# Fourth score chunk of the second attention layer by half products, in a four-layer graph network on one Trainium2 core

## The chip, the core and the metric

The kernel runs on one core of a Trainium2 chip. The core has a matrix engine (TensorE, PE in the profile, with its weight loads as PEld), three engines for elementwise work (VectorE or DVE, ScalarE or ACT, GpSimd or POOL), and SyncE (SP), which here only issues DMA transfers. Sixteen DMA engines move data between the chip's large memory (HBM, "DRAM" below) and the on-chip memory (SBUF); TensorE writes its results to PSUM. Each engine runs its own instructions in their order and waits for others through semaphores.

The metric is device time in microseconds (us). Before the change it was 2243.39 us, the median of six runs from 2237.05 to 2248.49.

## The reference

A graph has N = 2708 nodes with 512 features each and a symmetric 0/1 adjacency matrix `adj`. Four layers follow each other, each of the form `x = layernorm(x + layer(x, adj))`. Layers 0, 1 and 3 multiply `adj` by the features and then by a 512 x 512 weight. Layer 2 is the one that matters here. It holds two attention layers of this form:

```python
proj = x @ W
Wh, Ws = jnp.split(proj, 2, axis=-1)
scores = Wh @ Ws.T
a = jax.nn.softmax(scores, axis=-1) * adj
out = a @ Wh
out = out + x
return jax.nn.leaky_relu(out, NEG_SLOPE)
```

The scores are dense (2708 x 2708, 512 deep), and so is the sum of the softmax. The weighing `a @ Wh` is sparse, since `adj` has some 16 neighbours a node.

## The kernel before, in words

**Layout.** Nodes stand in 22 blocks of 128 rows (the last has 20 rows), and in six column chunks `CH` of 512, 512, 512, 512, 384 and 276 columns, numbered 0 to 5; "the fourth chunk" is number 3. Chunk k of an attention layer computes the scores of all 22 row blocks against its columns, transposed: a tile `s` of 128 x 512 for every row block.

**A chunk of scores, directly.** `scores` makes a block by four matmuls of 128 x 128 by 512 columns, accumulated in PSUM; ScalarE copies the result to SBUF. Block 21 (20 rows) is done in small tiles and summed by VectorE.

**A chunk of scores by seven half products.** Where the chunk's number stands in `SEVEN` (one list for each of the two attention layers, line 507), `pair_steps` takes two row blocks at a time and makes their scores from seven products of half the depth and half the columns instead of eight (Winograd's form of Strassen's method). There are ten such pairs; block 18 (`ALONE`) and block 21 are done directly. A product is two matmuls of 256 columns (`product`). The method needs sums and differences of both sides: of the weights side they are the tiles s1, s2 and s4 of each group of blocks, of the moving side t1, t2 and t4 (`sum_moving`). In the course of this ScalarE copies six parts out of PSUM (`spx`, `spy`, `u`, `v`), and VectorE adds `u` and `v` to them (`first_block`, `second_block`). For groups 0 to 3 the sums on the weights side don't stay in SBUF: chunk 0 writes them to DRAM (`keep_sums`), and each later chunk by seven loads them again (`load_sums`, three transfers of 256 KB a group, on SP's queue). `replace` and `restore` turn one quarter of the weights in place into a difference, and back to the original when the next chunk is direct.

**What goes on beside the scores.** While the scores of chunk k are made, chunk k-1 (and what is left of chunk k-2) goes through three more steps, recorded by the loop in `layer`:

1. Softening (`soften`, called through `soften_next`): VectorE subtracts the greatest score, ScalarE takes the exponential, VectorE adds to the running sum and multiplies by the mask, and SP stores the block in a DRAM table of rows (`pairs<-s`). A chunk takes 26 steps. The table alternates between two copies, so chunk k can't be stored before chunk k-2 has been read.
2. Gathering (`fetch`): when all of a chunk's blocks are stored, GpSimd issues indirect DMAs (`g<-pairs,givers`) that bring the rows of the neighbours. A full chunk has 48 of them, each into one of ten buffers.
3. Weighing (`weigh`): TensorE multiplies the gathered weights and features (`acc<-g`), one matmul for each gather; the first of a chunk is preceded by the divisors (`den`). `end` then does the rest of the block on VectorE.

**What sets the order.** The order of issue on every engine is that of recording (class `Ordered`). A clock in the recording code (`advance`) adds up TensorE's matmuls; `weigh` records a weighing only when by this clock its gather should have landed, unless it is called with `wait=True`. In `layer`, after each block ("end") a number `many` of softening steps is recorded, and one more step at each "mid" of `pair_steps`. With `old` for chunk k-1:

```python
many = 2 if self.to_soften[:1] == [old] else 3
if ch.seven:
    many = (many - 1 if n % 2 else many - 2) if k > 1 else 0
```

After the last chunk of the second attention layer the loop goes on with layer 3 (`early`, the `fill` of `layer`): eight stretches of adjacency matmuls (`acc<-m,xh` and `acc<-m,xl`). Before its first two, `early` calls `need(GROUPS[t + 2][1] - 1)`, which asks for finished rows 8 to 11 and then 12 to 15 and records weighings with `wait=True` until they are there. Rows 12 to 15 are those of chunk 3. They are then loaded from DRAM by `load_rows`, while rows 16 to 21 are taken from the SBUF tiles in `made`.

Of the kernel before, what the change touches and what calls it, by code (L numbers as in the profile page):

```python
# [27 lines left out]
CH = [(0, 512), (512, 512), (1024, 512), (1536, 512), (2048, 384), (2432, 276)]  # L28

GROUPS = [(0, 4), (4, 8), (8, 12), (12, 16), (16, 19), (19, 22)]  # L30
# [473 lines left out]
APART = 3  # L504
SOFT = NB + APART + 1
ALONE = 18
SEVEN = ([0,1,2,3],[0,1,2])
PROJECTED = [0, 1]


# [42 lines left out]
class Fast:  # L553
# [91 lines left out]
    def early(self, run):  # L645

        seq = run.seq
        yield True
        self.load(*seq[0])
        yield True  # L650
        self.load(*seq[1])
        self.prepare(*seq[0])
        yield True
        for t in range(4 * TWO):
            ly, k, g = seq[t]

            for later in seq[t + 2 if t == 0 else t + 6 : t + 7]:
                self.load_bytes(*later)
            if t < 2:
                self.attention.need(GROUPS[t + 2][1] - 1)  # L660
            self.load(*seq[t + 2])
            if t == 4:
                self.load_weights(ly)
            if t == 4 * TWO - 1:
                self.attention.need(GROUPS[4][1] - 1)
                for j in range(*GROUPS[4]):
                    ly.rows[j] = self.attention.made[j]
            self.prepare(*seq[t + 1])
            if g == 3:
                ly.begun[k] = []  # L670
            for n, j in enumerate(range(*GROUPS[g])):
                if t == 0:
                    self.multiply(ly, k, g, [j])
                else:
                    self.multiply(ly, k, g, ds=[n])
                if g == 3:
                    b = self.page(f"begun{k}_{n}")
                    self.nc.scalar.copy(b[:, : CH[k][1]], ly.acc[k][n][:, : CH[k][1]])
                    ly.begun[k].append(b)
                self.attention.advance(2 * cost(CH[k][1]))  # L680
                yield True
# [169 lines left out]
    def load(self, ly, k, g):  # L851

        c0, cw = CH[k]
        if (k, g) in ly.loaded:
            return
        ly.loaded.add((k, g))
        js = range(*GROUPS[g])
        if ly.number == 0:
            tiles = []
            for j in js:  # L860
                if k == 0:
                    self.load_rows(ly, j)
                at = self.wide(f"at{ly.number}_{k}_{j}")
                tiles.append(at)
                if j < NB - 1:
                    self.nc.sync.dma_start(
                        at[:, :cw], self.k.adj_t[bass.ts(j, P), c0 : c0 + cw]
                    )
                    continue

                few = self.k.adj_t[j * P : j * P + QW, c0 : c0 + cw]
                for d in range(DC):
                    self.nc.sync.dma_start(at[d * QW : (d + 1) * QW, :cw], few)
            ly.done["at", k, g] = tiles
        else:
            self.load_bytes(ly, k, g)
        if k == 0 and ly.number == 3 and g < 4:
            for j in range(*GROUPS[g]):
                self.load_rows(ly, j)
        if ly.number == 0 and g == (2 if k else 4):  # L880
            xt = [self.page(f"xt{k}_{c}") for c in range(DC)]
            for c in range(DC):
                self.nc.gpsimd.dma_start(xt[c][:, :cw], self.k.x_t[:, c, c0 : c0 + cw])
            ly.done["xt", k] = xt
# [744 lines left out]
class Attention:  # L1629
# [470 lines left out]
    def pair_steps(self, ch):  # L2100
# [52 lines left out]
        for n, p in enumerate(pairs):  # L2153
            self.replace(ch.ly, p[0])
            if ch.k == 0 and p[0] in groups and p[1] == 0:
                self.keep_sums(ch.ly, p[0])
            if ch.k and p[1] == 0 and p[0] + 1 in groups:
                self.load_sums(ch.ly, p[0] + 1)
            t = begin(n, p)
            ahead(t)  # L2160
            if old:
                first_block(old)
            yield "mid"
            one(t)
            if older:
                four(older)
            if following and p == pairs[-2]:
                self.load_sums(ch.ly, 0)
            yield "end"
            if old:  # L2170
                seven(old)
            yield "mid"
            six(t)
            if old:
                second_block(old)
            older, old = old, t
            yield "end"
# [371 lines left out]
    def layer(self, ly, chunks, fill):  # L2549
        f = self.f  # L2550
        self.chunks, self.made = chunks, {}
        for k, ch in enumerate(chunks):
# [3 lines left out]
            n = -1  # L2556
            for what in self.walk(ch):
                if what == "mid":
                    self.soften_next()
                    self.weigh()  # L2560
                    continue
                n += 1
                if old and n < old.masks_ahead:
                    self.load_mask(old, n)
                if not following and n > NB - 1 - ch.masks_ahead:
                    self.load_mask(ch, n - NB + ch.masks_ahead)
                if old and n < 2:
                    self.greatest(old, last=n == 1)
                if old and n == 2:
                    self.shift_rows(old)  # L2570
                many = 2 if self.to_soften[:1] == [old] else 3
                if ch.seven:
                    many = (many - 1 if n % 2 else many - 2) if k > 1 else 0
                for _ in range(many):
                    self.soften_next()
                f.beat()
                if k == 0 and n < NB:
                    self.copy_z(ly, n)
                if n == 14 and k:
                    f.packed(k - 1)  # L2580
                if following and n == 15:
                    self.load_moving(following)
                if following and following.seven and n == 18:
                    self.sum_moving(following)
                if not following and n in (5, 11, 19):
                    next(fill)
                if ch.seven and not following.seven and n >= 7 and n % 4 == 3:
                    self.restore(ly, n // 4 - 1)
                if not ch.seven and n == 1:
                    for i in sorted(ly.sums):  # L2590
                        self.restore(ly, i)
                self.greatest(ch)

                for _ in range(3):
                    if not self.weigh():
                        break
                late = k == 2 or ly.number == 0 and k == len(CH) - 1
                if old and n == (6 if late else 4):
                    self.shift_columns(old)
                    self.to_soften.append(old)  # L2600
        assert not self.to_soften
# [129 lines left out]
```

## Time and profile before

| What | us |
|---|---|
| median of six runs | 2243.39 |
| profiled execution | 2240.0 |
| its span, first to last instruction | 2238.3 |
| TensorE busy in it | 2186.1 (98%) |
| VectorE busy | 1627.2 (73%) |
| ScalarE busy | 825.7 (37%) |
| GpSimd busy | 719.3 (32%) |

Stages of the two attention layers in that execution, by the first score product of each chunk (us from the start of the span):

| Chunk | first layer | second layer | scores by seven in (first, second) |
|---|---|---|---|
| 0 | 735.03 | 1414.95 | both |
| 1 | 801.59 | 1479.13 | both |
| 2 | 867.52 | 1545.06 | both |
| 3 | 962.31 | 1640.18 | first only |
| 4 | 1064.94 | 1745.53 | neither |
| 5 | 1145.02 | 1829.29 | neither |
| work after the scores | 1204.19 | 1892.18 | |

The last weighing of the second layer ends at 2039.6.

How to read the profile: its rows group instructions by engine and by the names of the tiles that are written and read (`out<-in`). One f32 matmul appears as two records, so `x40` of scores are twenty matmuls. A matmul's busy time includes waiting once it has begun, so the distance between starts is used for prices. Nearly all rows have line L71, that of the recording helper; the names tell them apart.

### The profile page before, as it was taken

The page shows a single profiled execution, that of the slowest core. Times are in us where ns is not written, and L with a number is a line of the kernel's source. Part 1 is how long each engine was busy: PE and PEld are TensorE (multiplying, and loading weights), DVE is VectorE, ACT ScalarE, POOL GpSimd, SP SyncE. Part 2 cuts the span into 40 slices and gives each one's busy share as a digit, 9 for nine tenths or more (in the row PEclk, how much of TensorE's full clock was granted, in tenths as well). Part 3 has the DMA queues.
Part 4 walks back from the last instruction along what each step waited for, and adds up shares of the span by engine and source line. Part 5 has one row for each costly group of instructions (what it writes and reads, how often), then busy time and mean ns, then how long its engine had stood idle before and what let it go on. Part 6 is the DMA issues. An engine that isn't in the chain of part 4 may idle for free. (4 is left out here: it accounts for less than half of the span.)

```text
span 2238.3 us, 30631 instructions
## 1 busy us (share of the span) xinstructions
PE 2186.1 (98%) x10012; PEld 1572.6 (70%) x10012; DVE 1627.2 (73%) x3425; ACT 825.7 (37%) x1855; POOL 719.3 (32%) x827
## 2 busy tenths in 40 slices
PE   9999999999999999999999999999999999899997
PEld 6777778889887887666555666887643455477896
DVE  6777888897887869888867732459988688445744
ACT  7444363333333345343322422335432223442121
POOL 2333431111000000646566542000556556443000
PEclk9999999999999999999999999999999999999999
DMA  9976762222412855999899974764999899884221
GB/s 348 279 205 173 201 182 68 86 86 91 154 58 96 288 176 154 343 306 338 263 359 338 320 239 156 241 230 148 320 309 313 277 337 312 321 267 129 94 87 43
DMA packets 311566, 488.95 MB, mean 218 GB/s; under 512 B 37498, under 2 KB 178074, under 8 KB 311396
## 3 DMA queue, kind: packets, MB, share of 16 engines
q1 hardware_dynamic: 242740, 271.74, 36.8%
q0 software_dynamic: 68656, 215.15, 29.6%
q8 instruction: 81, 1.33, 0.2%
q14 instruction: 89, 0.73, 0.1%
HBM read 357.28 MB, written 162.76 MB: 232 GB/s over the span
## 5 line engine op out<-in xcount | busy, mean ns | idle before, releaser
L71 POOL DMA_INDIRECT g<-pairs,givers x510 | 537.5, 1054 | 799.4 <-DMA pairs<-s 224.1
L71 PE MATMUL acc<-m,xh 128*128 128x512 f32 (+4 forms) x1584 | 563.4, 377 | 1.0 <-issue 1.0
L71 PE MATMUL acc<-m,xl 128*128 128x512 f32 (+4 forms) x1584 | 549.7, 365 | 3.6 <-DVE xl L71 3.6
L71 PEld LDWEIGHTS acc<-m,xh 128*128 128x128 f32 (+1 forms) x1584 | 288.4, 188 | 59.8 <-issue 19.1
L71 PEld LDWEIGHTS acc<-m,xl 128*128 128x128 f32 (+1 forms) x1584 | 288.7, 188 | 46.0 <-DVE xl L71 4.1
L71 PE MATMUL sp<-xs,wst_sb 128*128 128x384 f32 (+2 forms) x960 | 300.0, 485 | 0.0
L71 PE MATMUL acc<-g 128*32 128x512 f32 (+1 forms) x1020 | 277.6, 611 | 9.2 <-DMA g<-pairs,givers 4.5
L71 PEld LDWEIGHTS sp<-xs,wst_sb 128*128 128x128 f32 x960 | 165.7, 182 | 131.1 <-issue 70.2
L71 ACT CAST m<-at 128x512 fp32r<-128x512 uint8 (+5 forms) x396 | 201.5, 567 | 115.3 <-DMA at<-mask 47.0
L71 PEld LDWEIGHTS acc<-g 128*32 128x32 f32 (+1 forms) x1020 | 77.2, 135 | 138.3 <-issue 108.6
L71 DVE TENSOR_TENSOR s<-s,a 128x512 f32<-128x512 f32 (+3 forms) x264 | 166.3, 630 | 9.1
L71 DVE TENSOR_TENSOR sum<-sum,s 128x512 f32<-128x512 f32 (+4 forms) x252 | 156.6, 621 | 10.2 <-issue 6.0
L71 DVE TENSOR_TENSOR s<-s,shift 128x512 f32<-128x512 f32 (+3 forms) x264 | 161.4, 620 | 1.9 <-ACT rs_t L71 1.1
L71 DVE TENSOR_TENSOR top<-top,s 128x512 f32<-128x512 f32 (+3 forms) x240 | 149.4, 623 | 15.7 <-ACT s L71 10.1
L71 ACT ACTIVATE s<-s 128x512 f32<-128x512 f32 (+3 forms) x264 | 146.5, 580 | 37.5 <-DVE s L71 22.6
L71 ACT COPY s<-sp 128x384 f32<-128x384 f32 (+2 forms) x112 | 52.7, 472 | 267.6 <-PE sp L71 176.7
L71 ACT COPY s<-spx 128x256 f32<-128x256 f32 x210 | 77.9, 373 | 144.6 <-PE spx L71 115.2
L71 POOL DMA_DIRECT2D x<-o x44 | 25.6, 589 | 324.5 <-DVE o L71 281.0
L71 PE MATMUL spx<-xs,wst_sb 128*128 128x256 f32 x400 | 103.2, 382 | 4.6 <-issue 2.1
L71 DVE SCALAR_TENSOR_TENSOR xr<-acc,rden,xr 128x512 f32<-128x512 f32 (+1 forms) x44 | 32.7, 744 | 93.1 <-PE acc L71 61.4
L71 PE MATMUL mm<-w,ht 128*128 128x512 f32 (+1 forms) x240 | 100.1, 594 | 0.0
L71 PEld LDWEIGHTS spx<-xs,wst_sb 128*128 128x128 f32 x400 | 75.1, 190 | 26.5 <-issue 11.4
(349 smaller groups left out, 3320.5 us busy)
## 6 DMA issues: line engine op xcount, KB each, us to landing
pairs<-s SPq DMA_DIRECT2D x168, 256.0 KB
at<-in_adj_t SPq DMA_DIRECT2D x84, 256.0 KB
pairs<-pairs SPq DMA_DIRECT2D x42, 512.0 KB
s<-sums SPq DMA_DIRECT2D x60, 256.0 KB
xres<-x POOLq DMA_DIRECT2D x44, 256.0 KB
x<-o POOLq DMA_DIRECT2D x43, 256.0 KB
pairs<-z_sb SPq DMA_DIRECT2D x42, 256.0 KB
pairs<-pairs SPq DMA_DIRECT2D x42, 256.0 KB
```

The lines of the kernel that those rows point to most:

```text
L71: ins = call(*args, **kw)
```

## The change

`SEVEN` gets chunk 3 for the second attention layer as well. Besides, group 1 of the sums is loaded at the end of the chunk before and no longer at the beginning of the chunk that uses it; the number of softening steps after a block is 2 for all chunks, and 1 or 2 in turn in the last one; the shift of chunk 4 is recorded two blocks earlier in the last chunk of the first layer (block 4, not 6); and rows 12 to 15 of layer 3 are taken from `made`, not loaded.

```diff
-SEVEN = ([0,1,2,3],[0,1,2])
+SEVEN = ([0,1,2,3],[0,1,2,3])
...
             if t < 2:
                 self.attention.need(GROUPS[t + 2][1] - 1)
+            if t == 1:
+                for j in range(*GROUPS[3]):
+                    ly.rows[j] = self.attention.made[j]
             self.load(*seq[t + 2])
...
-        if k == 0 and ly.number == 3 and g < 4:
+        if k == 0 and ly.number == 3 and g < 3:
             for j in range(*GROUPS[g]):
                 self.load_rows(ly, j)
...
-            if ch.k and p[1] == 0 and p[0] + 1 in groups:
+            if ch.k and p[1] == 0 and p[0] > 0 and p[0] + 1 in groups:
                 self.load_sums(ch.ly, p[0] + 1)
...
-            if following and p == pairs[-2]:
-                self.load_sums(ch.ly, 0)
+            if following and p in pairs[-2:]:
+                self.load_sums(ch.ly, pairs.index(p) - len(pairs) + 2)
...
-                many = 2 if self.to_soften[:1] == [old] else 3
+                many = 1 + n % 2 if k == len(CH) - 1 else 2
                 if ch.seven:
                     many = (many - 1 if n % 2 else many - 2) if k > 1 else 0
...
-                late = k == 2 or ly.number == 0 and k == len(CH) - 1
-                if old and n == (6 if late else 4):
+                if old and n == (6 if k == 2 else 4):
                     self.shift_columns(old)
                     self.to_soften.append(old)
```

The instructions of the two programs, counted by chunk in the order in which they stand: in the second layer's chunk 3, 80 score matmuls of 512 columns go and 140 of 256 columns come. Weighings recorded in a chunk's stretch change like this:

| Stretch | first layer, before and after | second layer, before and after |
|---|---|---|
| chunk 2 | 38, 26 | 38, 26 |
| chunk 3 | 54, 62 | 58, 62 |
| chunk 4 | 42, 46 | 48, 46 |
| chunk 5 | 30, 30 | 38, 30 |
| after the scores | 91, 91 | 73, 91 |

In the second layer, 10 weighings of chunk 3 stood after the scores; now 28 do. The 16 weighings of chunk 4 that `need` records with `wait=True` stand right behind them in both programs. The divisors of chunk 3, which open its weighing, stood behind 28 score matmuls of chunk 5 and now stand behind 52.

## The prediction

> **What bounds the kernel now.** I read the page first, then busy time by stage, then waits and the timeline of the stages that change.
>
> ```profile
> span 2238.3 us, 30631 instructions
> ...
> PE 2186.1 (98%) x10012; PEld 1572.6 (70%) x10012; DVE 1627.2 (73%) x3425; ACT 825.7 (37%) x1855; POOL 719.3 (32%) x827
> ...
> PEclk9999999999999999999999999999999999999999
> DMA  9976762222412855999899974764999899884221
> ```
>
> TensorE is busy 98% of the span, so fewer matmuls should shorten it. But DMA is at 9 tenths exactly in the two stretches of attention, so a gather may be what TensorE waits for there. The stages (start:end, length, then PE, PEld, DVE, ACT, POOL busy, clock, DMA share, GB/s) separate these. First the second layer's chunks 1, 2 and 3, then the first layer's chunk 3, which is already made by seven products:
>
> ```profile
> 1479.13:1545.06 65.93, 65.93 (x305) 55.55 (x304) 52.67 (x91) 31.12 (x75) 0.00 (x0) 1.00 0.44 139
> 1545.06:1640.18 95.12, 87.72 (x389) 61.98 (x388) 85.95 (x145) 38.59 (x91) 45.69 (x43) 1.00 0.85 286
> 1640.18:1745.53 105.35, 104.87 (x313) 42.08 (x312) 89.58 (x151) 28.70 (x51) 60.67 (x57) 1.00 0.94 307
> ```
> ```profile
> 962.31:1064.94 102.63, 97.62 (x437) 65.99 (x436) 83.58 (x139) 38.10 (x90) 55.20 (x53) 1.00 0.97 322
> ```
>
> Chunk 1 is pure TensorE. Chunk 3 made directly leaves TensorE idle for 0.5 us; made by seven products, in the first layer, for 5.0. Chunk 2 idles 7.4. Its two longest waits, in TensorE's timeline:
>
> ```profile
> 1566.14 1.13 PE L71 MATMUL spx<-t,wst_sb 128*128 128x256 f32 x4 [1.75 <-ACT v L71]
> 1579.68 1.13 PE L71 MATMUL spy<-t,s 128*128 128x256 f32 x4 [2.47 <-DMA s<-sums]
> ```
>
> The last stretch that matters lies after the scores, where `need` records weighings without regard to their gathers:
>
> ```profile
> 1909.35 5.37 PE L71 MATMUL acc<-g 128*128 128x512 f32 x8 [1.00 <-DMA g<-pairs,givers]
> 1915.14 6.27 PE L71 MATMUL acc<-g 128*32 128x512 f32 x12 [0.42 <-issue]
> ...
> 1928.08 1.13 PE L71 MATMUL acc<-g 128*128 128x512 f32 x2 [0.28 <-issue]
> ```
>
> From 1909.35 to 1928.64 TensorE does only the 16 forced weighings of chunk 4. Eight whole ones at 0.89 (1680.06 to 1682.72 for three) and two lists of four quarters at 1.0 are 9.1 us; the stretch takes 19.3. Ten us are lost here and count as busy. The sixteenth gather is issued at 1922.1: **this point is set by the stream of gathers, not by TensorE.** Afterwards adjacency matmuls cover nearly everything to the end.
>
> **The change, part by part.** The sums are made against the profiled execution, 2240.0 us (span 2238.3 and 1.7 around it), which lies 3.4 under the median of 2243.39.
>
> *Matmuls.* A direct score matmul costs 0.860 us (1682.72 to 1686.16 for four), a half one 0.432 (1549.36 to 1550.22 for two). 80 x 0.860 = 68.8 go, 140 x 0.432 = 60.5 come: **-8.3 us of TensorE's work**, all in chunk 3 of the second layer.
>
> Here a rule speaks against the change. The row first: half matmuls stand 0.216 us apart a record, and the weight load of each takes 0.190 beside it. The Trainium skill, "TensorE: Matmul & The Clock Gate", section "Back-to-back issue gap", says that in a stream of weight loads and matmuls both set the spacing, and that with few columns the formula for a single matmul counts too little (81 ns against 56 at 128 columns). An estimate from that page, 25 ns on each of 280 records, is 7 us, and the gain would be 1.3. The rows show no such surcharge, so -8.3 stands.
>
> *What seven products need on other engines in that chunk.* VectorE gets 10 additions `s<-s,u` at 0.684, 9 `s<-s,v` at 0.419 and two subtractions more: 6.8 + 3.8 + 0.8 = 11.4 us. ScalarE exchanges 19 copies of 512 columns at 0.586 for 29 `s<-spx`, 9 `v`, 10 `s<-spy` at 0.373 and 10 `u` at 0.593: +12.7 us on 28.7 busy of 105, which is hidden. VectorE's is hidden only if it can run near full: 89.6 busy and some 10.7 more (busy time there is 0.935 of the sum of its durations) are 100 in a stage of 100. The first layer's chunk 3 shows what this costs, 5.0 of TensorE idle in place of 0.5: **+4.5**, bounded by 0 below and 10 above (VectorE at the 90% of chunk 2: 100/0.90 = 111 for the stage).
>
> *Sums.* Twelve loads of 256 KB more, 3.1 MB; at the stage's 307 GB/s that is 10 us of all sixteen engines, in a stage at 0.94 of them. SP issues them between the pair stores. Bounds: 0, if they fall into the 6% that is free, to +9, if every gather moves. I take +1, since the first layer's chunk 3 carries the same load at 0.97 and its gathers go on.
>
> *Sums a chunk ahead.* The wait of 2.47 above is for group 2. In SP's order its three loads stood behind eight pair stores, and SP waits 36.6 us for VectorE in that stage; the group 1 loads, now gone to the chunk before, and the slower softening leave four of those stores behind it instead of ahead. **-2.5** in the second layer, **-0.7** in the first (the same wait is 0.74 there). If the loads are still late, 0.
>
> *Fewer softening steps.* No step goes away; they are moved. In chunk 2 of both layers VectorE gets relief where it is densest (98% busy from 1550 to 1600). TensorE's other idle time there, 4.9 and 5.5 us, should halve: **-2.5 in each layer** (0 to -5). The price is that chunk 0's gathers begin later: its divisors stand behind 104 score matmuls of chunk 2, not 82, and 12 weighings move to chunk 3. GpSimd idles 10 us between chunks 0 and 1, so this lag has room; without the room it costs up to 5. Queued behind the moved steps are only the pair stores on SP and the gathers on GpSimd.
>
> *Order in chunk 5.* Here the gain is handed back. The divisors of chunk 3, and so the weighing that frees the ten gather buffers, stand behind 52 score matmuls of chunk 5, not 28: 24 x 0.478 (1863.95 to 1867.77 for eight) = 11.5 us later in TensorE's work. So -8.3 before it becomes **+3.2** there; with -5.0 from chunk 2, +4.5 and +1, the first weighing of chunk 3 comes about 3.7 later than at 1843.46. From the gather behind it (1844.84) to the sixteenth of chunk 4 the stream takes 77.3 us for 52, 1.49 each. An unhindered gather takes 1.26 (0.95 and 0.30 idle), a mean one 1.37 (207 from 1575.7 to 1922.1, less 62 us in which GpSimd waited for stores and buffers). Now that the weighings are forced, buffers come free at once. At 1.37 it is 71.2, **-6.1**; at 1.26, -11.8; at 1.49, 0. The forced point comes 6.1 - 3.7 = **2.4 us earlier**, and TensorE waits longer in front of it: what was gained in matmuls is spent there.
>
> *Rows 12 to 15 from SBUF.* Four loads of 256 KB go. VectorE waited 4.13 us for them at 1947.20, but TensorE had adjacency matmuls: 0, at best -2. *Shift two blocks earlier* in the first layer's last chunk: 2 blocks of slack for VectorE, 0.
>
> **Sum.** Second layer -2.4; first layer -0.7 - 2.5 = -3.2, which its tail keeps, as its projections follow on TensorE without forced weighings. Together -5.6: 2234.4 for an execution like the profiled one, **2238 us** on the scale of the median.
>
> **Rivals.**
>
> 1. *The whole saving arrives.* If gathers keep 1.26 and chunk 3 costs no new idle time, the forced point moves by 3.2 - 5.0 - 11.8 = -13.6; with -3.2 of the first layer -16.8: **2227**. For it: ten us of forced waiting is room for TensorE. Against: DMA share of 0.94 there.
> 2. *VectorE becomes the bound in chunk 3* (slower). If it gets no further than 90%, the stage takes 111 and not 101; chunk 2's pair stores, chunk 3's and then every gather move with it, and the forced point comes at 10 - 2.4 = +7.6. The first layer's gain then falls too, for the same reason, to about 0: with a gather or two more in the tail **2252**. It decides from the point at which the stage exceeds its old 105. For it: 85.95 of 95.12 in the densest stage. Against: 98% over 50 us.
> 3. *Nothing happens to the time.* The later gathers of chunk 0 cost what the shorter waits gain, in both layers, and the forced point stays: **2243**. For it: TensorE loses its time at gathers whatever it does before.
>
> **Chances.** Forecast 0.41 (2232 to 2244), rival 1 0.27 (2222 to 2232), rival 2 0.17 (2250 to 2258), rival 3 0.15 (2240 to 2248). A measurement of this kernel can tell about 0.3% from no change, 6.7 us; 2236.7 is the border. Faster is rival 1 and a little over a third of the forecast, 0.27 + 0.16 = 0.43; slower rival 2 with 0.17; the same 0.40. The range reaches into both rivals: 2225 to 2252.
>
> **What would show it.** Right: the row `spy<-t,s` loses its wait for sums; the second layer's chunk 3 takes 98 to 104 us with TensorE idle some 5 of it; the chunk 3 divisors come within 5 us of the old place after 1414.95; the forced stretch begins earlier and is longer. Wrong: chunk 3 above 105 with VectorE over 95% (rival 2), gathers of chunk 3 and 4 at 1.26 and the forced stretch shorter (rival 1), or the first layer no shorter from 735.03 to 1414.95 (its -3.2).

## The result and the profile after

The changed kernel takes 2259.13 us (median of 35 runs, 2239.4 to 2274.41) where the kernel before takes 2244.94 on the same chip (72 runs, 2233.64 to 2265.08): a ratio of 1.0063, 95% interval 1.005 to 1.0076. It is **14 us slower**, and lies above the range of the prediction (2225 to 2252). The profiled execution took 2258.96, its span 2257.2.

The page of the changed kernel, the lines that answer to those shown of before:

```profile
span 2257.2 us, 30965 instructions
...
PE 2186.8 (97%) x10132; PEld 1601.8 (71%) x10132; DVE 1637.4 (73%) x3453; ACT 836.6 (37%) x1895; POOL 720.1 (32%) x827
...
PEclk9999999999999999999999999999999999999999
DMA  9976752223322945999989873855989899874221
```

TensorE is as busy as before (2186.1 there), although the change takes 8 us of matmuls away. So some 9 us more of it are waits that count as busy, or matmuls at half clock (the mean granted clock is 0.990 here and 0.995 before), and outside its busy time it stands still for 70.4 us in place of 52.2 (span less busy). Busy time by stage, in the columns of the prediction: the second layer's chunks 2 and 3, then the first layer's chunk 3.

```profile
1549.93:1643.74 93.81, 82.63 (x365) 61.38 (x364) 86.46 (x148) 37.84 (x90) 35.49 (x34) 0.95 0.81 273
1643.74:1749.38 105.64, 100.66 (x437) 65.56 (x436) 90.98 (x158) 39.31 (x89) 64.54 (x61) 1.00 0.93 315
951.11:1059.47 108.36, 102.57 (x454) 67.72 (x452) 91.51 (x150) 40.16 (x93) 68.07 (x61) 0.98 0.98 332
```

Chunk 3 of the second layer takes 105.6 as before, with 5.0 of TensorE idle. Chunk 2 now idles 11.2 (7.4 before) and has half clock in it. TensorE's timeline there; a row without brackets had no wait:

```profile
1579.23 1.03 PE L71 MATMUL spy<-t,s 128*128 128x256 f32 x4
...
1635.55 2.07 PE L71 MATMUL spy<-xs,wst_sb 128*128 128x256 f32 x4 [10.96 <-ACT s L71]
```

The wait for sums (2.47 at `spy<-t,s`) is gone, and a wait of 11 us for ScalarE has come. Yet chunks 4 and 5 are shorter, and the second layer's scores end 467.8 us after its start, 6.7 earlier than before. All of it is lost behind the scores. First TensorE waits for VectorE's `xl` (the part of the features that `xh` leaves), in front of the second adjacency matmul; at this place there was no such wait before:

```profile
1894.61 0.79 PE L71 MATMUL acc<-m,xl 128*128 128x512 f32 x1 [6.73 <-DVE xl L71]
```

Then comes the stretch in which it does nothing but weighings. Its first row before, then the changed kernel:

```profile
1904.62 2.97 PE L71 MATMUL acc<-g 128*32 128x512 f32 x8
```
```profile
1908.61 4.00 PE L71 MATMUL acc<-g 128*32 128x512 f32 x16
1913.25 6.41 PE L71 MATMUL acc<-g 128*128 128x512 f32 x12 [0.64 <-issue]
...
1926.94 1.05 PE L71 MATMUL acc<-g 128*32 128x512 f32 x2 [1.91 <-DMA g<-pairs,givers]
...
1938.42 2.04 PE L71 MATMUL acc<-g 128*32 128x512 f32 x4 [1.66 <-DMA g<-pairs,givers]
1940.67 7.49 PE L71 MATMUL acc<-g 128*32 128x512 f32 x16 [0.20 <-issue]
```

Before, it lasted 24.0 us, from 489.7 to 513.7 after the layer's start (19.3 of them for the 16 weighings of chunk 4); now it lasts 39.0, from 488.8 to 527.8. The last weighing ends 638.6 after the layer's start, where it was 624.6; what follows takes 198.8 and 198.7. So 14 us come in between the second layer's start and its last weighing (the other 5 of these two executions lie ahead of that start), and the question is why the gathers are late.

Followed back, the gathers are late from chunk 2's first on. That one needs chunk 2's last block, the one of 20 rows, to be softened and stored. First the kernel before: the last multiplication by the mask on VectorE, then the gather on GpSimd.

```profile
1727.54 0.68 DVE L71 TENSOR_TENSOR s<-s,a 20x512 f32<-20x512 f32 x1
```
```profile
1742.19 0.95 POOL L71 DMA_INDIRECT g<-pairs,givers  x1 [7.37 <-PE acc L71]
```

The same two of the changed kernel:

```profile
1756.73 0.68 DVE L71 TENSOR_TENSOR s<-s,a 20x512 f32<-20x512 f32 x1
```
```profile
1760.42 0.95 POOL L71 DMA_INDIRECT g<-pairs,givers  x1 [7.08 <-DMA pairs<-s]
```

Counted from each layer's start (1414.95 and 1419.82), this last multiplication began at 312.6 and now begins at 336.9. Before, GpSimd waited for a weighing to free its buffer (`PE acc`), with the chunk long softened: the gather came 14.6 us after the multiplication. Now it waits for the store (`DMA pairs<-s`) and comes 3.7 after it, so 11 of the 14.6 were slack. **24.3 us of delay ate the 11 of slack, and 13.4 show**: the first gather moves from 327.2 to 340.6.

The delay doesn't run straight on from there. Chunk 3's first gather comes only 5.5 later (412.1 and 417.6), since chunk 3 is softened no later than before (407.9 and 405.3). The 156th gather of the layer, the twelfth of chunk 3, is 11.9 late again (429.9 and 441.8). It waits for a weighing to free a buffer, and chunk 3's first weighing stands behind the divisors, which come at 439.6 in place of 427.5. Before, then changed:

```profile
1844.84 1.00 POOL L71 DMA_INDIRECT g<-pairs,givers  x1 [3.82 <-PE acc L71]
```
```profile
1861.59 1.19 POOL L71 DMA_INDIRECT g<-pairs,givers  x1 [7.72 <-PE acc L71]
...
1899.49 0.99 POOL L71 DMA_INDIRECT g<-pairs,givers  x1 [6.81 <-PE acc L71]
```

The last row is a second such wait, for a weighing that stands behind the adjacency matmuls that waited for `xl`. The sixteenth gather of chunk 4 then moves from 507.2 to 523.1 and the last of all from 616.6 to 632.3. So the trace shows two places at which TensorE's weighings hold up the stream of gathers, behind the divisors of chunk 3 and behind `xl`.

Why is chunk 2's softening later? The code has it. Beside a direct chunk it goes 2 steps a block, so 26 steps take 13 blocks. Beside a chunk by seven, `many - 1` or `many - 2` in turn and one step at each "mid" make 1.5 a block, so they take 17.3: 4.3 blocks of 4.8 us later, some 21 us. Besides, VectorE has 11 us of additions more.

### The profile page after: what moved, and what is told of

It reads as the page before. It is cut to its first block, busy times and chain, and to the rows that moved or that the text cites. A ratio compares the mean times of both kernels' runs of the same rounds, so it can differ in the third digit from the quotient of the medians.

```text
span 2257.2 us, 30965 instructions
## 1 busy us (share of the span) xinstructions
PE 2186.8 (97%) x10132; PEld 1601.8 (71%) x10132; DVE 1637.4 (73%) x3453; ACT 836.6 (37%) x1895; POOL 720.1 (32%) x827
## 5 line engine op out<-in xcount | busy, mean ns | idle before, releaser
L71 PE MATMUL acc<-g 128*32 128x512 f32 (+1 forms) x1020 | 283.0, 614 | 11.5 <-DMA g<-pairs,givers 6.6
L71 PE MATMUL sp<-xs,wst_sb 128*128 128x384 f32 (+5 forms) x800 | 228.8, 462 | 0.6 <-DVE s L71 0.6
L71 PEld LDWEIGHTS sp<-xs,wst_sb 128*128 128x128 f32 (+1 forms) x800 | 136.3, 181 | 90.9 <-issue 32.8
L71 ACT COPY s<-spx 128x256 f32<-128x256 f32 x240 | 88.5, 373 | 165.1 <-PE spx L71 115.2
L71 PE MATMUL spx<-xs,wst_sb 128*128 128x256 f32 x480 | 122.9, 381 | 0.0
L71 PEld LDWEIGHTS spx<-xs,wst_sb 128*128 128x128 f32 x480 | 90.5, 190 | 25.9 <-issue 11.1
L71 ACT COPY s<-sp 128x384 f32<-128x384 f32 (+2 forms) x92 | 40.5, 445 | 177.7 <-PE sp L71 92.9
```

Source lines behind the costliest of these rows:

```text
L71: ins = call(*args, **kw)
```

## The experiments

Ratios are to the kernel before on the same chip. That kernel took 2209 to 2211 us in the runs beside e5 to e8, e17 and e18, and 2243 to 2252 beside the others, so traces are compared only where both belong to the same group, unless said otherwise. All times are of the second layer, in us after its start, in one profiled execution each (those of e1 and e9 lie 16 to 17 us under the medians of their runs): the beginning of chunk 2's last multiplication ("softened"), chunk 2's first gather, and the divisors of chunk 3, with the number of chunk 5's score matmuls that stand in front of them.

| Run | What differs | Ratio, 95% interval | Softened | Gather | Divisors (matmuls) |
|---|---|---|---|---|---|
| kernel before | | | 312.6 | 327.2 | 427.5 (28) |
| changed kernel | | 1.0063 (1.005 to 1.0076) | 336.9 | 340.6 | 439.6 (52) |
| e1 | seven products alone | 1.0094 (1.0062 to 1.0125) | 334.3 | 337.9 | 438.8 (52) |
| e2 | fewer softening steps and shift alone | 1.0002 (0.9978 to 1.0025) | 311.9 | 321.2 | 423.9 (32) |
| e3 | change with old softening | 1.0086 (1.0057 to 1.0116) | 338.0 | 341.6 | 440.9 (52) |
| e4 | change, sums not ahead | 1.0082 (1.0054 to 1.011) | 337.1 | 340.8 | 443.5 (52) |
| e5 | e1, faster softening in chunk 3 | 1.0034 (1.002 to 1.0047) | 313.2 | 326.9 | 427.4 (32) |
| e6 | e1, without additions | 1.0057 (1.0045 to 1.0069) | 331.5 | 335.2 | 435.8 (52) |
| e7 | before, with VectorE work added | 1.001 (1.0001 to 1.0019) | 312.1 | 324.2 | 421.5 (28) |
| e8 | before, chunk 3 direct in both layers | 1.0052 (1.0036 to 1.0068) | 312.3 | 323.1 | 424.4 (28) |
| e9 | change, moving sums late | 1.0054 (1.003 to 1.0077) | 328.1 | 331.9 | 435.5 (52) |
| e10 | change, faster softening in chunk 3 | 1.0041 (1.0016 to 1.0066) | 319.1 | 334.5 | 447.2 (32) |
| e11 | both, in both layers | 1.0062 (1.0039 to 1.0085) | 308.8 | 322.7 | 433.9 (32) |
| e12 | e11 with old softening elsewhere | 1.007 (1.0042 to 1.0098) | 312.5 | 328.5 | 434.6 (32) |
| e13 | e9 and e10 | 1.0029 (1.0006 to 1.0052) | 310.5 | 327.2 | 438.8 (32) |
| e14 | e13 with old softening elsewhere | 1.0062 (1.0038 to 1.0086) | 314.4 | 331.1 | 441.8 (32) |
| e15 | e2, moving sums late | 0.9999 (0.9973 to 1.0025) | 312.5 | 322.1 | 430.6 (32) |
| e16 | before, three pages held | 0.9975 (0.9953 to 0.9996) | 322.1 | 331.9 | 433.7 (28) |
| e17 | before, twelve loads added | 0.9998 (0.9988 to 1.0007) | 311.2 | 325.2 | 423.2 (28) |
| e18 | e5 and e6 together | 0.9993 (0.9984 to 1.0001) | 307.6 | 322.9 | 423.9 (32) |

### Which part of the change: e1 to e4

The first theory (A) laid it to the fewer softening steps. The rivals were the seven products themselves (B) and the sums that lie in SBUF a chunk ahead (C).

e1:

```diff
-SEVEN = ([0,1,2,3],[0,1,2])
+SEVEN = ([0,1,2,3],[0,1,2,3])
```

> Only the seven products of the second layer's chunk 3 come; softening, shift, sums and rows are those of the kernel before. Theory A (slower softening makes the first gather of every chunk and so the whole stream of gathers later; the seven products are what the prediction says): 5 us faster, -10 to -1, the second layer's last weighing no later than +624.65 after its start. Theory B (the seven products do it, by VectorE and DMA in chunk 3 or by the divisors of chunk 3 that come behind more matmuls of chunk 5): 10 to 14 us slower. Theory C (sums a chunk ahead hold SBUF pages that the stored blocks need): as theory A, but chunk 2 of the second layer without the wait of 11 us that ScalarE's copies cause.

e2, against the kernel before:

```diff
-                many = 2 if self.to_soften[:1] == [old] else 3
+                many = 1 + n % 2 if k == len(CH) - 1 else 2
...
-                late = k == 2 or ly.number == 0 and k == len(CH) - 1
-                if old and n == (6 if late else 4):
+                if old and n == (6 if k == 2 else 4):
```

> Only the fewer softening steps and the earlier shift come; the second layer's chunk 3 is made directly and the sums are loaded as before. Theory A: 6 to 12 us slower, 3 to 4 of them in the first layer, whose chunks 0 to 3 are those of the changed kernel but for the sums. Theory B: 5 faster to 1 slower. Theory C: 3 faster to 2 slower, since no sums lie in SBUF ahead of their chunk.

e3, against the changed kernel:

```diff
-                many = 1 + n % 2 if k == len(CH) - 1 else 2
+                many = 2 if self.to_soften[:1] == [old] else 3
```

> The changed kernel with the number of softening steps of before; all else of the change stays. Theory A: 5 to 10 us faster than before the change, so 20 less than the changed kernel. Theory B: 10 to 14 slower, as the changed kernel. Theory C: 3 to 8 slower, with a wait of TensorE for ScalarE's copies in chunk 2 of the second layer that is longer than 3 us.

e4, against the changed kernel:

```diff
-            if ch.k and p[1] == 0 and p[0] > 0 and p[0] + 1 in groups:
+            if ch.k and p[1] == 0 and p[0] + 1 in groups:
...
-            if following and p in pairs[-2:]:
-                self.load_sums(ch.ly, pairs.index(p) - len(pairs) + 2)
+            if following and p == pairs[-2]:
+                self.load_sums(ch.ly, 0)
```

> The changed kernel with the sums of group 1 loaded in their own chunk, as before. Theory A: 8 to 14 us slower than before the change, like the changed kernel. Theory B: the same. Theory C: between 5 faster and 3 slower, and the wait of 11 us in chunk 2 of the second layer gone.

Theory A fell at once. The seven products alone cost 21 us of 2243 (14 to 28), as much as the whole change or more; the softening alone costs nothing, 0.0% with 0.2 to either side. Theory C fell with e4, and B stands, though e1 cost more than its 10 to 14. The table shows its mark: wherever the second layer's chunk 3 is made by seven products at the old pace, chunk 2 is softened at 328 to 338 and not at 312. The difference of e3 and the changed kernel (1.0086 and 1.0063) leans towards a gain of 5 us from the fewer steps, and that of e4 towards 4 from the sums ahead; the intervals overlap, and neither is shown.

### Why: pace or VectorE, e5 to e7, e17, e18

Two explanations were left: the branch for seven products records the softening more slowly (O), or VectorE's 19 additions push it back (V).

e5, against e1:

```diff
                     many = (many - 1 if n % 2 else many - 2) if k > 1 else 0
+                    if ly.number and k == 3:
+                        many += 1
```

> Seven products alone, as in e1, with one softening step more after each block of the second layer's chunk 3. The first gather of chunk 2 came 327.2 us after the layer's start before and 337.9 in e1. Theory V (VectorE has 11 us of additions more to do ahead of chunk 2's last stores): it stays at 334 or more, TensorE waits longer in chunk 3, and the kernel is 10 to 20 us slower than before the change, like e1 (19). Theory O (the branch for seven products records chunk 2's softening steps more slowly, so its stores and gathers come later and the weighings fall behind): it comes at 325 to 331, and the kernel is between 5 faster and 4 slower than before.

e6, against e1, with `bare` true in the second layer's chunk 3:

```diff
         def first_block(t):
-            nc.vector.tensor_add(t["s"][:, :cw], t["s"][:, :cw], t["u"][:, :cw])
+            if not bare:
+                nc.vector.tensor_add(t["s"][:, :cw], t["s"][:, :cw], t["u"][:, :cw])
...
-            nc.vector.tensor_add(t["r"][:, h:cw], t["r"][:, h:cw], t["v"][:, :h])
+            if not bare:
+                nc.vector.tensor_add(t["r"][:, h:cw], t["r"][:, h:cw], t["v"][:, :h])
```

> Seven products alone, as in e1, without the 19 additions of u and v on VectorE in the second layer's chunk 3; those scores are then wrong. Theory V: first gather of chunk 2 at 325 to 331 after the layer's start, 3 to 12 us faster than before the change. Theory O: still 334 or later, 10 to 18 slower. Both in part: between them.

e18 has both edits:

> Seven products alone with the faster softening of e5 and without the 19 additions of e6; the scores of that chunk are then wrong. e5 was 7.5 us slower than before, e6 12.7. If the pace of softening and VectorE's additions are the whole loss: 7 faster to 1 slower than before, which is the forecast's gain in matmuls. Theory D, or another cost of seven products: 3 to 8 slower still.

With e1, these make a table of two by two, in per cent over the kernel before:

| | additions made | additions left out |
|---|---|---|
| softening at 1.5 a block | +0.94 | +0.57 |
| softening at 2.5 a block | +0.34 | -0.07 |

The pace is worth 0.60 and 0.64, 13 to 14 us; the additions 0.37 and 0.41, 8 to 9 us. The differences against e18 are good to 0.16, those against e1 only to 0.34, so that the two add up is no more than likely. Even so **O is the larger part and V the smaller**; e5's 7.5 us lay between the two ranges that had been set for it. In the traces: e6, without additions, still has its first gather behind a late chunk. VectorE's last softening of chunk 2 and GpSimd's timeline in e6:

```profile
1729.21 0.68 DVE L71 TENSOR_TENSOR s<-s,a 20x512 f32<-20x512 f32 x1
```
```profile
1732.90 0.95 POOL L71 DMA_INDIRECT g<-pairs,givers  x1 [8.69 <-DMA a<-mask]
```

The releaser given is a mask load that landed at that time. But the gather is issued 3.0 us after the end of the last softening, exactly as in e1 (1745.37 to 1748.38) and in the changed kernel (1757.41 to 1760.42), where the store is named. In e5, at the higher pace, the softening ends 13 us before the gather, and GpSimd goes on from chunk 1's gathers without a wait:

```profile
1710.53 0.68 DVE L71 TENSOR_TENSOR s<-s,a 20x512 f32<-20x512 f32 x1
```
```profile
1724.21 1.26 POOL L71 DMA_INDIRECT g<-pairs,givers  x1 [0.30 <-PE spy L71]
```

The pace also sets where the divisors stand. In all six kernels that make chunk 3 by seven at the old pace (the changed one, e1, e3, e4, e6, e9) they stand behind 52 score matmuls of chunk 5, and in all six the first matmul with `xl` waits 5.2 to 7.8 us behind the scores. With faster softening they stand behind 32, with a direct chunk behind 28 or 32, and no wait at that place is over 3.4. e6 and e18 differ by the pace alone: with the pace of e18 chunk 2's first gather comes 12.3 earlier, chunk 3's first 6.0, its divisors 11.9, the sixteenth gather of chunk 4 16.0 and the last weighing 15.0. What the divisors' place and the wait for `xl` cost apart was not tested.

e7 adds VectorE's work to a direct chunk:

```diff
         nc.scalar.copy(s[:n, :cw], ps[:n, :cw])
+        if ch.ly.number == 1 and ch.k == 3 and j != ALONE:
+            if ch.last is not None:
+                w = cw if ch.extra % 2 == 0 else cw // 2
+                nc.vector.tensor_max(ch.last[:, :w], ch.last[:, :w], ch.last[:, :w])
+                ch.extra += 1
+            ch.last = s
```

> The kernel before, its chunk 3 of the second layer made directly, with 19 operations of two operands more on VectorE there (s = max(s, s), in turn over 512 and 256 columns, some 10.6 us), which change no value. Theory V: chunk 2's first gather some 10 later, 8 to 14 us slower than before. Theory O: 0 to 3 slower, since the order of softening is that of before.

It cost 2 us, not 8 to 14. The same work beside a direct chunk fits into the slack in front of the first gather (softened at 312.1, gather at 324.2), so it isn't VectorE's time as such that costs 8 to 9 beside seven products. e17 adds the loads alone:

```diff
+                if (ly.number, k) == (1, 3) and n in (1, 5, 10, 15):
+                    g = (1, 5, 10, 15).index(n)
+                    for i in range(3):
+                        t = self.page(f"more{g}_{i}", FP, (P, 2, 2 * P))
+                        self.nc.sync.dma_start(t, self.sums[1][g][i])
```

> The kernel before with twelve loads of 256 KB of the sums in the second layer's chunk 3, which nothing reads, issued in four groups after blocks 1, 5, 10 and 15 as seven products would need them. Theory D (the loads take what the gathers need, in a stage in which the DMA engines are busy 94%): 4 to 9 us slower than before; the gathers of chunk 2 come later by as much. Otherwise 0 to 2 slower.

Twelve loads cost nothing (0.9998), at a DMA share of 0.98. Chunk 3 of the second layer in e17 (direct), e5, e6 and e18 shows what TensorE really saves:

```profile
1620.19:1723.48 103.29, 103.29 (x313) 42.10 (x312) 86.22 (x146) 28.77 (x51) 60.16 (x57) 1.00 0.98 344
```
```profile
1628.57:1727.67 99.10, 93.75 (x421) 63.81 (x420) 92.49 (x161) 39.58 (x90) 58.65 (x54) 1.00 0.97 328
```
```profile
1631.84:1727.37 95.53, 93.20 (x421) 63.97 (x420) 81.12 (x137) 39.28 (x89) 54.20 (x50) 1.00 0.97 322
```
```profile
1627.08:1721.70 94.62, 93.36 (x421) 64.23 (x420) 83.35 (x142) 39.98 (x90) 57.92 (x54) 1.00 0.98 335
```

TensorE is busy 9.9 us less in e18 than in e17. Of that 1.0 (at the prediction's price) is a list of four quarter weighings, which the stage of e17 has and the others lack (58 weighings and 54); 8.9 are the score matmuls. In e5 its idle time is 5.4, in e18, without additions, 1.3. And yet e18, with the matmuls saved and both losses taken out, takes as long as before (0.9993; 1.5 us less, within noise). Chunk 3 begins 4.7 later in it than in e17 (231.3 and 226.6 after the layer's start), and its sixteenth gather of chunk 4 comes at 501.0, in e17 at 500.7. **In these two traces the second layer ends with its gathers, whatever TensorE saved in chunk 3.**

### The other layer: e8

```diff
-SEVEN = ([0,1,2,3],[0,1,2])
+SEVEN = ([0,1,2],[0,1,2])
```

> The kernel before with chunk 3 made directly in the first layer too. If the stream of gathers is what seven products cost (V or O), the first layer's first gather of chunk 2 comes at 327 after the layer's start, not at 338, and what TensorE pays (8.3 us of matmuls less 4.5 of waits) is given back behind the scores: 0 to 8 faster. If the first layer's end follows TensorE's matmuls, 3 to 6 slower.

In the first layer the gathers behave as in the second: chunk 2's first comes at 324.2 in e8 and at 330.4 in e7 and e17, the last of all at 598.2 and not 602.3. But the kernel gets 11.5 us slower, more than either range. The first layer's chunk 3, in e8 and then in e7:

```profile
959.89:1066.00 106.11, 106.11 (x329) 43.98 (x328) 73.91 (x116) 27.87 (x52) 59.27 (x59) 1.00 0.90 303
```
```profile
960.78:1058.46 97.68, 95.82 (x437) 65.87 (x436) 83.96 (x137) 39.10 (x91) 54.98 (x52) 1.00 0.98 333
```

8.4 us more there, and 10 by the start of the second layer (668.1 after the first's start, 658.1 in e7). So in the first layer the seven products bring some 11 us. The reason offered, that TensorE's own work counts there because it still has the projections for the second layer to do behind the scores, is an argument from the code; no run took them away.

### The pages: e9, e16, and both cures: e10 to e15

The wait of 11 us in chunk 2 was the next suspect. In the changed kernel ScalarE's copies stand behind `DMA pairs<-s` there, that is, behind the store that frees an SBUF page:

```profile
1626.97 0.59 ACT L71 COPY u<-spy 128x512 f32<-128x512 f32 x1 [5.05 <-DMA pairs<-s]
1635.13 0.37 ACT L71 COPY s<-spy 128x256 f32<-128x256 f32 x1 [7.57 <-DMA pairs<-s]
```

The Trainium skill, "Perfetto Trace Analysis", section "Optimization Strategy", says that repeated bubbles on the engine that should be saturated can mean that buffers have run out. This one doesn't repeat, but it is such a bubble; e9 takes it away.

```diff
-                if following and following.seven and n == 18:
+                if following and following.seven and n == (21 if k == 2 else 18):
                     self.sum_moving(following)
```

> The changed kernel with the moving side's sums (t1, t2, t4: three SBUF pages) of chunk 3 made after the last block of chunk 2 and not after its nineteenth, in both layers. The change cost 14 us. Theory P (in chunk 2 the pages run out; ScalarE's copies wait until stored blocks free one, TensorE behind them, and the clock is halved after the wait): the wait of 11 us in the second layer's chunk 2 falls under 4, less half clock, 3 to 9 us slower than before instead of 14. Theory Q (that wait is VectorE's or ScalarE's own work): the wait stays, or goes to the start of chunk 3 with the six subtractions, 12 to 17 slower.

The wait fell to 3.1, chunk 2 to 85.7 us, and the time hardly moved (1.0054, some 12 us over before, and so outside the 3 to 9 of theory P):

```profile
1547.18:1632.86 85.68, 82.33 (x366) 61.05 (x365) 82.10 (x139) 36.33 (x86) 35.63 (x33) 0.98 0.80 274
```

e16 holds the three pages without seven products:

```diff
-                if following and following.seven and n == 18:
+                if following and n == 18 and (following.seven or (ly.number, k) == (1, 2)):
                     self.sum_moving(following)
+                if (ly.number, k) == (1, 3) and n == 4:
+                    for m in ("t1", "t2", "t4"):
+                        t = ch.part[m][0]
+                        self.nc.vector.tensor_max(t, t, t)
```

> The kernel before with the moving sums of the second layer's chunk 3 made after the nineteenth block of chunk 2, though chunk 3 is direct and doesn't use them, and read once on VectorE in chunk 3: three pages are held, some 3 to 4 us of VectorE added, nothing else. Theory PC: ScalarE's copies in chunk 2 wait 3 us or more for a stored block, TensorE behind them, and the kernel is 3 to 8 slower than before, at least half of it half clock. Otherwise: 0 to 2 slower.

TensorE has no wait of 3 us in chunk 2 (ScalarE one of 3.3 for a store), and there is no loss (0.9975; the profiled execution, with its later gather, was one of the longer ones). So the pages explain the bubble only together with the rest of the change, and the bubble isn't what the change costs: without it the time is the same within noise (e9). e10 is e5's edit on the changed kernel, e11 adds e9's and has the pace in both layers, e12 has the old `many` besides, e13 the pace in the second layer alone, e14 is e13 with the old `many`, e15 is e2 with e9's edit.

> The changed kernel with one softening step more after each block of the second layer's chunk 3 (e5's edit on the whole change). If the late gathers of chunk 2 are a loss of their own besides the pages: 4 to 9 us slower than before in place of 14, chunk 2's first gather under 335 after the layer's start in place of 340.6, and the wait of 11 us in chunk 2 as long as in the changed kernel. If the lateness comes from the wait in chunk 2 alone: 12 to 16 slower.

> The changed kernel with both edits, the moving sums late and the faster softening, in chunk 3 of both layers. If pages and pace are the two losses and add up: between 6 faster and 3 slower than before the change. If VectorE is the bound once the pace is higher: 5 to 12 slower, with TensorE waiting in chunk 3 for VectorE's u and v additions.

> As e11, but with the number of softening steps of before in all other chunks. If fewer steps are a gain once pages are free (e2 was 8 us shorter apart from the clock): 4 to 8 us slower than e11. If they only move waits: within 3 of e11.

> The changed kernel with the moving sums late in both layers and the faster softening in the second layer's chunk 3 alone. Theory PC (two losses: gathers that come later by the pace, and waits for pages after which the clock is halved): span times clock, that is the time without the halved clock, 8 to 15 us under that of the changed kernel, and the whole between 4 faster and 5 slower than before the change. Theory R (the clock is lost to whatever fills TensorE's queue more tightly, not to the page wait): span times clock 8 to 15 under, but as much half clock as in the changed kernel or more, 5 to 11 slower than before.

> As e13, with the number of softening steps of before elsewhere. Theory PC: half clock as before the change within 4 us, span times clock 0 to 5 over before; between 0 and 7 slower. Theory R: the same, 0 to 7 slower; if it is over 9 slower, the faster softening of chunk 3 isn't the cure that e5 showed.

> e2 (fewer softening steps alone, chunk 3 direct in the second layer) with the moving sums of the first layer's chunk 3 late. In e2 span times clock was 8 us under before, and the halved clock took 8 back. Theory PC: part of that half clock comes from page waits in the first layer's chunk 2, so 2 to 8 us faster than before. Theory R: as e2, within 2 of before.

The pace brings the change from 14 us to 9 (e10), and with the late sums to 6.5 (e13, interval 1 to 12): what e5 kept, 7.5, is left here too. The intervals overlap with that of the changed kernel; those of e5 and e1 do not. In both layers it doesn't help (e11, e12): in e11's profile the first layer's scores end 488.5 after its start, 19 later than before. e11 and e14 are slower than expected; e14 above all, at 14 us where 0 to 7 was expected and over 9 was to speak against the cure. It differs from e5 by the sums ahead, the late moving sums, the rows and the shift. In e10, e13 and e14 the divisors stand behind 32 matmuls as in e5, and yet come at 439 to 447: TensorE idles 21 to 29 us in front of them (15.8 in e5), 5 to 8 of it in chunk 4, where it idles 0.0 in e5. e12 lies within 3 us of e11, as one of its two ranges said. e15 stays at the time of before, against theory PC. No version beat the kernel before beyond doubt: e16's 0.9975 has no mechanism behind it, and e18 leaves work out.

## Why the prediction was wrong, step by step

**The step that failed** is "Order in chunk 5": "the first weighing of chunk 3 comes about 3.7 later". The divisors in front of it came 12.1 later after the layer's start (427.5 to 439.6; 11.3 in e1). TensorE's time from the layer's start to the divisors, before and then changed:

```profile
1414.95:1842.45 427.50, 418.09 (x1648) 263.83 (x1647) 335.24 (x585) 150.20 (x329) 164.69 (x155) 1.00 0.84 279
```
```profile
1419.82:1859.40 439.58, 422.19 (x1815) 297.28 (x1814) 353.72 (x626) 166.80 (x381) 166.03 (x155) 0.99 0.83 279
```

The matmuls in front were priced rightly, at +3.2 (busy +4.1 here, with half clock in it). The waits were not. They stood at -5.0 from chunk 2, +4.5 and +1; TensorE's idle time grew by 8.0, from 9.4 to 17.4. Chunk 3's part is the 4.5; but chunk 2's idle time rose from 7.4 to 11.2. The sum had no term for what seven products in chunk 3 cost in chunk 2: chunk 3 begins 4.2 later in e1 than before, and 4.7 later in e18 than in e17. Nor did the step ask why the divisors stand behind 52 matmuls. That place goes with chunk 2's softening, which is recorded 21 us later beside seven products; at a higher pace it is 32. e5, e6 and e18 show what this costs: 13 to 14 us by the pace, 8 to 9 by the additions.

- *The stream recovers* (77.3 to 71.2 us, -6.1): wrong. From its 156th gather to the 208th it took 81.3. Buffers did not come free at once: GpSimd waited 14.8 us for weighings in it (6.4 before), 6.8 of them behind the wait for `xl`, which the sum did not have. So the forced point came 15.9 later, not 2.4 earlier. The forced stretch did begin earlier (by 0.9) and last longer, but with late gathers and 18 more weighings of chunk 3 behind the scores.
- *Matmuls* (-8.3): right, 8.9 by e17 and e18. The surcharge of 25 ns a record, an estimate from the Trainium skill ("TensorE: Matmul & The Clock Gate", section "Back-to-back issue gap"), isn't in these rows.
- *Other engines in chunk 3* (+4.5): TensorE's idle time there is 5.0, as priced. But VectorE's additions cost the kernel 8 to 9 by e5 and e18; the price for TensorE's waits alone was half of it. The stage took 105.6, not 98 to 104: four more weighings stand in it (62, not 58).
- *Sums* (+1): 0 by e17. *Sums a chunk ahead* (-2.5): the wait went, the gain didn't show (e4).
- *Fewer softening steps* (-2.5 in each layer): 0.0 us by e2, 5 to either side. Chunk 2 did get shorter (88.6 in e2, 95.1 before), but in these two traces the sixteenth gather of chunk 4 comes no earlier (509.1 and 507.2).
- *First layer* (-3.2): 683.5 in place of 679.9 in the profile. The rows can't carry a difference of 3 us, since the same first layer took 676.2 in e1 and 694.9 in e16.
- *Rows from SBUF* and *shift* (0): nothing in e2 or e3 speaks against it.
- *Rivals.* The sign of rival 2 was right and the start of its chain (chunk 2's stores, then its gathers), its condition wrong: the stage hardly exceeded 105 (105.6; 98.6 in e1), and VectorE got no fuller than 86 to 90%. Chunk 3's stores did not move with it. Softening went late in the order, not only slowly. Rival 3's reason, that TensorE loses at the gathers whatever it does before, fits e18.

The profile of before held the answer. Its first layer made chunk 3 by seven products already. There, chunk 2's first gather came 337.9 us after the layer's start, and chunk 3's divisors at 440.9, behind 52 score matmuls of chunk 5; in the second layer, with a direct chunk, at 327.2 and 427.5, behind 28. The prediction read that stage for TensorE's idle time (5.0) and did not ask when its gathers began.

What stays open: why the additions cost 8 to 9 us beside seven products and 2 beside direct ones (that there the next blocks wait for them is an argument, not a measurement; in the profiled executions the last weighing comes at 614.8 in e5 and 611.6 in e18, only 3 apart), how the loss by the pace divides between the divisors' place and the wait for `xl`, and why e14 kept nothing of e5's cure, where e10 and e13 kept some. The mean granted clock was 0.989 in the runs of the changed kernel and 0.994 in those of before (beside e4); if all of the difference were work lost, it would be 11 us. It can't be told apart from the waits that it follows; in e2 and e15 the clock was as low (0.991 and 0.989) at the time of before.

## What to carry to other kernels

Where a later stage is fed in order by a chain over several engines, price a change by the time at which each link of the chain ends and by the slack behind it, not by the busy time of the engine that gains. Ask of each branch that a change newly enters what else it paces: here a list entry also slowed the softening from 2 steps to 1.5 a block, and put the divisors behind 52 matmuls in place of 28. And if another part of the same kernel already runs in the new way, read all its marks in the profile of before, the first transfer of the next stage above all.

## What the runs showed of the hardware

- The granted clock drops to half in stretches of 3.41 us or multiples of it. The stretch around the long wait of the changed kernel, with TensorE busy 3.53 of 10.24 us at clock 0.50:

```profile
1628.84:1639.08 10.24, 3.53 (x8) 2.52 (x8) 9.30 (x17) 1.97 (x5) 1.92 (x3) 0.50 0.99 352
```

  Two thirds of it lie in the wait itself and cost nothing. The Trainium skill, "TensorE: Matmul & The Clock Gate", section "What's actually happening", gives a free-running window of 3413 ns; its length agrees. At the wait for sums (`spy<-t,s` in chunk 2), 2.11 us were followed by half clock in e1, and 2.47 us were not in the kernel before.
- Twelve loads of 256 KB in a stage with the DMA engines 0.94 to 0.98 busy cost nothing that could be measured (e17, 0.9998, 0.9988 to 1.0007).
- The kernel before took 2209 to 2211 us on two chips and 2243 to 2252 on the others. In the traces the difference lies in the layers with gathers: the first layer took 658.1 in e7 and 679.9 in the profile of before, with the same instructions in it.
